# A graph network's first pass over the edges: later scans of a block's sums, and another deal of the last block's columns between TensorE and GpSimd

## The chip, the cores and the metric

The kernel runs on one core of a Trainium2 chip. The metric is the device time of one execution in microseconds (us), as the median of several runs.

## The reference

6250 nodes with 16 features each are joined by 200,000 edges, given as `src` and `dst`, with `dst` in ascending order. Four layers follow each other; after each, the layer's result is added to `x`, and the rows are normalised. Cut to what the kernel's passes over the edges do:

```python
x = _layernorm(x + segment_sum(tanh(x[src] * edge_weight[:, None]), dst))           # layer 0: first pass
x = _layernorm(x + edge_attention(x, edge_attr_16, W_msg, W_attn, src, dst))        # layer 1: another kind of loop
h = segment_max(x[src] * edge_weight1, dst);  x = _layernorm(x + h @ W.T + b)       # layer 2: second pass
h = relu(gin_conv(x, ...));  h = gin_conv(h, ...)                                   # layer 3: third and fourth pass,
x = _layernorm(x + log_softmax(h))                                                  #   each a segment_sum(x[src], dst)
```

## The kernel before

**The layout.** 125 partitions hold 1600 consecutive edges each (`P` = 125, `J` = 1600), so one column of edges is 125 edges, one per partition. A pass (`edge_scan`, called four times, for layers 0, 2, and twice for layer 3) goes through 8 blocks (`NB`) of 200 columns (`JB`). For each block it fills a tile `xb` with the 16 features of every edge's source node, multiplies by weights where the layer has them (`message`; in the first pass with ScalarE's tanh after it), runs 16 scans along the columns, one per feature (`pieces`, L554 and L557), and stores the running sums (`keep_rows`) to DRAM, from where the values at each node's last edge are gathered later (`at_nodes`).

**Two ways to fetch the features.** GpSimd (POOL) fetches a column by an indirect DMA (`gather`, L100), one instruction for each column, all issued at the start of a block (L573 and L574). TensorE (PE) fetches the others by products: `one_hot` (L487; in the first pass its fourth part is made on ScalarE, L491 and L492) turns 12 columns of keys into one-hot matrices, `select` multiplies them for four columns at a time with the table of nodes in three bf16 parts and four groups of columns (48 matmuls, L523), and VectorE (DVE) picks the right entry out of PSUM with a product and a reduction (`kept`, L527, and L532). A batch is 12 columns (`BC`), three `select` calls, 144 matmuls. `select` has three PSUM buffers, `xb` has two.

**Who fetches what.** In blocks 0 to 6, PE fetches the first 120 columns (`NPE`, ten batches) and POOL the last 80. In block 7, the batches are dealt over the block: of every 16 columns (`LW`), PE fetches 12 and POOL 4, over 12 batches in the first pass (`more` = `MORE` = 24 columns on top of 120), over 11 in the second, over 10 in the last two. Columns after the last batch are POOL's. So POOL fetches 56 columns of block 7 in the first pass.

**The order of work.** The order of instructions is written out by hand (`tc.manual_schedule()`). Within the loop over batches, batch c = 0 of a block first issues POOL's gathers into a new `xb` buffer; these wait until the scans of the block two before have read that buffer. The block that was filled before is kept in `waiting`; its `message` stands at c = 2 of the next block (L580), and its 16 scans and its store follow in `todo`, two after each `select` from c = 3 on, so that they end at c = 5 (L602 to L605). Block 7 is scanned in parts, since nothing comes after it: at c = 5 the columns up to there (0 to 64), at the last batch the columns from 64 to that batch's first (176), and the rest after the loop (L586 to L615). `sc`, which the scans write, has one buffer; the next block's scans wait for its store.

**Work beside the first pass.** `prelude` attaches other steps of the program to the `select` calls of the first pass, by number (`at(k, ...)`, three numbers to a batch): keys of the later blocks (`keys_made`), the ends of the nodes' edges (with 51 gathers on POOL at number 50), rows of edges for layer 1 (`edge_rows`, from number 19 on, in steps), 50 scatters on POOL at number 102 (`chunks_put`), the chunk steps at 150 to 168 (`chunks_got` to `chunks_use`), and weights of later layers at 172 to 188.

Of the kernel before, what the change touches and what calls it, by code (L numbers as in the profile page):

```python
# [25 lines left out]
NB = J // JB  # L26
# [6 lines left out]
NPE = 120  # L33
GP = 125
BC = 12
MORE = 24
KEYED = NB * NPE + MORE
LW = 16
SG = 4
GROUPS = ((0, 13), (26, 12), (38, 12), (13, 13))  # L40
GR = len(GROUPS)
# [9 lines left out]
def tile_gnn_resnorm(ctx: ExitStack, tc: tile.TileContext, a: dict, out: bass.AP):  # L51
# [185 lines left out]
    def keys_made(sp, b):  # L237

        w = NPE if b < NB - 1 else NPE + MORE
        df = sp.tile([P, w], F32, name="key_df")  # L240
# [68 lines left out]
    def by_target(t):  # L309
        return t[bass.ds(half, E), :]  # L310
# [184 lines left out]
    def edge_scan(tag, table, parts, F, message, pen, tmp, beside=None, first=None, more=0):  # L495
# [7 lines left out]
        shared = beside is not None  # L503
# [4 lines left out]
        with tc.tile_pool(name=f"es_{tag}", bufs=3) as ep, \  # L508
# [4 lines left out]
            batches = [(b, c) for b in range(NB) for c in range(len(batches_of(b, more)))]  # L513
            lasts = len(batches_of(NB - 1, more)) - 1

            def select(xb, j, oh, k, c):

                all_ps = gp.tile([128, SG // 2, 512], F32, name="all_ps")
                for i in range(SG):
                    for g, (a0, n) in enumerate(GROUPS):  # L520
                        o = all_ps[:, i // 2, (i % 2) * W:(i % 2) * W + n * F]
                        for q in range(3):
                            nc.tensor.matmul(o, oh[:, g, (c + i) * P:(c + i) * P + 128],  # L523
                                             parts[:, q, a0:a0 + n, :].rearrange("p a f -> p (a f)"),
                                             start=(g == 0 and q == 0), stop=(g == GR - 1 and q == 2))
                kept = ep.tile([P, SG, GA, F], F32, name="kept", bufs=1)
                nc.vector.tensor_tensor(  # L527
                    kept.rearrange("p (h i) a f -> p h (i a) f", i=2),
                    all_ps[:P, :, :2 * W].rearrange("p h (i f) -> p h i f", f=F),
                    place1[:, k * BC + c:k * BC + c + SG, :].rearrange("p (h i) a -> p h (i a)", i=2).unsqueeze(3).to_broadcast(  # L530
                        [P, SG // 2, 2 * GA, F]), op=OP.mult)
                nc.vector.tensor_reduce(xb[:, j:j + SG, :], kept.rearrange("p i a f -> p i f a"), AX.X, OP.add)  # L532
# [34 lines left out]
            prev, todo, waiting = None, [], []  # L567
            for k, (b, c) in enumerate(batches):
                if c == 0:
                    xb_all = ep.tile([128, JB, F], F32, name="xb", bufs=2)  # L570
                    xb = xb_all[:P]
                    at = batches_of(b, more)
                    for j in sorted(set(range(JB)) - {j + i for j in at for i in range(BC)}):  # L573
                        gather(xb_all[:GP, j, :], table, src_all[:GP, b * JB + j:b * JB + j + 1])  # L574
                oh = ohs
                if keys:
                    ohs = one_hot(ep, keys.pop(0), shared=shared)
                if k + 2 < len(batches):
                    keys.append(load_keys(ep, k + 2))
                if c == 2 and waiting:  # L580
                    xw, bw = waiting.pop(0)
                    message(xw, bw, 0, JB)
                    sc, last = scans(bw, prev)
                    prev, todo = sc, pieces(xw, bw, sc, last, 0, JB)
                    todo.append(lambda sc=sc, bw=bw: keep_rows(sc, bw, 0, JB))
                if b == NB - 1 and c in (5, lasts):  # L586

                    while todo:
                        todo.pop(0)()
                    if c == 5:  # L590
                        sc, last = scans(b, prev)
                        lo, hi = 0, at[c - 1]
                    else:
                        lo, hi = hi, at[c]
                    message(xb, b, lo, hi)
                    todo = pieces(xb, b, sc, last, lo, hi)
                    todo.append(lambda lo=lo, hi=hi: keep_rows(sc, b, lo, hi))
                for i in range(0, BC, SG):
                    for do in beside.pop((k * BC + i) // SG, ()):
                        do()  # L600
                    select(xb, at[c] + i, oh, k, i)
                    if c > 2:  # L602
                        for do in todo[:6 if b == NB - 1 and c == lasts else 2]:
                            do()
                            todo.remove(do)  # L605
                if k + 1 == len(batches) or batches[k + 1][1] == 0:
                    while todo:
                        todo.pop(0)()
                    waiting.append((xb, b))
# [193 lines left out]
    def chunks_got(tmp, n, got):  # L803

        for i in range(n, min(n + 2, NC)):
            also = tmp.tile([128, Q, 4], F32, name="ck_also" if i else "ck_got", bufs=2 if i else 1)
            nc.sync.dma_start(also, chunk_d[i].rearrange("(p t) c -> p t c", t=Q))
            if i:
                nc.vector.tensor_max(got, got, also)
            else:  # L810
                got = also
        return got

    def chunks_last(tmp, got, cur):

        for f in range(4):
            nc.vector.tensor_tensor_scan(cur[:, :, f], got[:, :, f], got[:, :, f], 0.0, op0=OP.max, op1=OP.max)
        tail = tmp.tile([128, 4], F32, name="ck_tail")
        nc.vector.tensor_copy(tail, cur[:, Q - 1, :])
        nc.vector.tensor_scalar(nost, tail[:, 0:1], 0.0, None, op0=OP.is_equal)  # L820
        return tail

    def chunks_tail(scratch, tail):
        tail_ps = scratch(4, 128)
        nc.tensor.transpose(tail_ps, tail, ident)
        return tail_ps

    def chunks_run(tmp, tail_ps):
        tails = tmp.tile([4, 128], F32, name="ck_tails")
        nc.vector.tensor_copy(tails, tail_ps)  # L830
        run = tmp.tile([4, 129], F32, name="ck_run")
        nc.vector.memset(run[:, 0:1], 0.0)
        nc.vector.tensor_tensor_scan(run[:, 1:], tails, tails, 0.0, op0=OP.max, op1=OP.max)
        return run

    def chunks_before(scratch, run):
        before_ps = scratch(128, 4)
        nc.tensor.transpose(before_ps, run[:, :128], ident[:4, :4])
        return before_ps
# [54 lines left out]
    def attention_weights(tmp):  # L894
        w = tmp.tile([NK, D, 2, D], F32, name="w_am")
        for q in range(3):
            for k, n in enumerate(("attn", "msg")):
                nc.sync.dma_start(w[q * D:(q + 1) * D, :, k, :], a[f"L1_gnn_W_{n}"].rearrange("e (i o) -> e i o", o=D))
        for k, n in enumerate(("attn", "msg")):
            nc.sync.dma_start(w[3 * D:NK, :, k, :], a[f"L1_gnn_b_{n}"].rearrange("(x i o) -> x i o", x=1, o=D))  # L900
        return w

    def attention_parts(tmp, w):
        w_m = tmp.tile([NK, 2 * DD], BF16, name="w_m")
        nc.vector.memset(w_l, 0.0)
        w = w.rearrange("e i k o -> e (i k o)")
        split3(nc.vector.tensor_copy, w_h[:NK, :], w_m, w_l[:NK, :], w, w)
        nc.sync.dma_start(w_h[NK:, :], w_m)
        nc.vector.tensor_copy(identb, ident)
# [36 lines left out]
    def prelude(kp, more):  # L946
# [6 lines left out]
        now = {}  # L953

        def at(k, do):
            jobs.setdefault(k, []).append(do)
# [9 lines left out]
        def open_pool(name):  # L966
            stack.close()
            now["sp"] = stack.enter_context(tc.tile_pool(name=name, bufs=1))

        def put(**what):  # L970
            for k, f in what.items():
                now[k] = f
# [40 lines left out]
        at(100, lambda: put(c=chunks_set(now["sp"], *now["c"])))  # L1013
        at(102, lambda: chunks_put(*now["c"]))
        for i in range(0, NC, 2):
            at(150 + i, lambda i=i: put(got=chunks_got(now["sp"], i, now.get("got"))))
        at(160, lambda: put(c=chunks_last(now["sp"], now["got"], now["raw"])))
        at(163, lambda: put(c=chunks_tail(scratch, now["c"])))
        at(164, lambda: put(c=chunks_run(now["sp"], now["c"])))
        at(167, lambda: put(c=chunks_before(scratch, now["c"])))  # L1020
        at(168, lambda: chunks_use(now["sp"], now["got"], now["raw"], now["c"]))
        at(172, lambda: open_pool("weights"))
        at(172, lambda: put(w=attention_weights(now["sp"])))
        at(176, lambda: attention_parts(now["sp"], now["w"]))
        for i in range(3):
            at(180 + 4 * i, lambda i=i: node_weights(i))
        at(20, lambda: store(nc.sync, ew, by_target(ew_d).rearrange("(p j) o -> p (j o)", j=J)))
        at(14, lambda: put(r=edge_rows_begin(now["rp"])))
        for i in range(J // WE):
# [184 lines left out]
    with tc.tile_pool(name="l1t", bufs=1) as lp, tc.tile_pool(name="l1tp", bufs=1, space=PSUM) as pp:  # L1214
# [12 lines left out]
        for h in range(2):  # L1227
# [16 lines left out]
            now = lp.tile([128, 128], F32, name="now", bufs=2)  # L1244
# [240 lines left out]
```

## Time and profile before

| what | value |
|---|---|
| median of 8 runs | 8196.98 us (8185.38 to 8218.49) |
| the profiled execution's own time | 8247.67 us |
| its span, from first to last instruction | 8245.9 us |
| granted TensorE clock, mean | 0.958 |
| PE busy | 7207.2 us (87%) |
| DVE busy | 6757.2 us (82%) |
| POOL busy | 5803.9 us (70%) |
| ACT busy | 2158.3 us (26%) |
| first pass | 29.9 to 1348.1 us |
| layer 1 | 1348.1 to 4547.1 us |
| second, third and fourth pass | 4547.1 to 5756, to 6981, to 8245.9 us |

All times within the kernel are from one profiled execution, whose own time is 50.7 us above the median of the runs. An engine's busy share over the whole span is an average over stages with different limits, so the first pass has to be read for itself. "Idle before" a group of instructions, or a wait in the list of waits, names what ended the wait; "issue" means that the profile shows nothing that the engine waited for. PE's matmuls are pipelined, so a busy PE is not PE at its peak: the count of matmuls in a stretch tells the pace. Some matmul records can be missing.

### The profile page before, as it was taken

To read this page: it belongs to the slowest core of one execution; us is meant where nothing else is said; L and a number is where in the kernel's file an instruction comes from. 1 tells how busy PE (TensorE), PEld (TensorE's weight loads), DVE (VectorE), ACT (ScalarE), POOL (GpSimd) and SP (SyncE) were. 2 spreads that over 40 slices of the span, in tenths; PEclk is the share of its full clock that TensorE was granted. 3 is DMA by queue.
4 is the path that set the end of the run, shared out by engine and by line. 5 is a ranking of instruction groups with operands and counts; after the bars stand their busy time and mean duration, and the time that the engine had idled before them with its cause. 6 is when DMAs were issued, how large, how long until landed. Compare 5 with 4: busy or idle time off the path is not lost. (4 is left out here: it accounts for less than half of the span.)

```text
span 8245.9 us, 134767 instructions
## 1 busy us (share of the span) xinstructions
PE 7207.2 (87%) x56019; PEld 5194.4 (63%) x56019; DVE 6757.2 (82%) x7894; ACT 2158.3 (26%) x3387; POOL 5803.9 (70%) x4870
## 2 busy tenths in 40 slices
PE   7888895699999999999995899995999996999995
PEld 6786785244444444444442788985888885788884
DVE  8797875699999999999998687876687875677875
ACT  2343331355555555555555000000000000000000
POOL 6888753777777777777773787772787673877673
PEclk9999997899999999999997999997999997999997
DMA  4343432111211222221213122221222221122221
GB/s 132 88 108 91 105 84 72 39 49 49 52 49 49 50 51 50 51 52 49 52 49 124 35 50 41 50 40 31 37 50 41 49 42 35 31 50 40 49 41 29
DMA packets 288780, 461.34 MB, mean 56 GB/s; under 512 B 134741, under 2 KB 187270, under 8 KB 284358
## 3 DMA queue, kind: packets, MB, share of 16 engines
q1 hardware_dynamic: 122818, 332.42, 12.0%
q0 software_dynamic: 164880, 105.68, 11.0%
q10 hardware_dynamic: 448, 14.40, 0.5%
q8 instruction: 445, 7.29, 0.4%
q14 instruction: 189, 1.55, 0.1%
HBM read 257.45 MB, written 206.15 MB: 56 GB/s over the span
## 5 line engine op out<-in xcount | busy, mean ns | idle before, releaser
L523 PE MATMUL all_ps<-parts,oh 125*128 125x208 bf16 (+1 forms) x46512 | 4393.9, 250 | 365.4 <-issue 142.6
L523 PEld LDWEIGHTS <-oh 125*128 125x128 bf16 x46512 | 3945.3, 98 | 813.2 <-issue 724.0
L100 POOL DMA_INDIRECT hg<-table_x,g x1760 | 2024.2, 1150 | 546.2 <-issue 514.5
L100 POOL DMA_INDIRECT xb<-table_x,src x1268 | 1595.4, 1258 | 539.0 <-issue 413.9
L527 DVE TENSOR_TENSOR kept<-all_ps,place 125x832 f32<-125x832 f32 x969 | 986.1, 1018 | 897.1 <-remote 783.9
L1146 PE MATMUL la<-e,ident 128*128 128x512 f32 x3520 | 1576.5, 601 | 4.5 <-DVE e L1133 3.8
L532 DVE TENSOR_REDUCE xb<-kept 125x64 f32<-125x832 f32 x969 | 1521.1, 1570 | 33.3
L1146 PEld LDWEIGHTS la<-e,ident 128*128 128x128 f32 x3520 | 659.5, 193 | 753.2 <-issue 746.2
L1098 DVE TENSOR_TENSOR e<-mm,hg 128x1024 f32<-128x1024 f32 x880 | 1016.3, 1210 | 126.9 <-remote 80.6
L100 POOL DMA_INDIRECT xb<-table_l3b,src x640 | 793.3, 1240 | 301.4 <-issue 216.4
L100 POOL DMA_INDIRECT xb<-in_x,src x616 | 787.1, 1278 | 265.2 <-issue 232.2
L1093 PE MATMUL mm<-w_h,eT 98*128 98x512 bf16 x1760 | 675.3, 384 | 340.5 <-DVE e L1098 155.6
L1110 ACT ACTIVATE e<-e,epen 128x256 f32<-128x256 f32 x1760 | 786.8, 500 | 134.9 <-issue 98.6
L487 DVE TENSOR_SCALAR oh<-keys,mykey 125x1504 bf16<-125x1504 uint16 x1202 | 741.2, 676 | 46.7 <-DMA keys<-key_d 27.6
L1094 PE MATMUL mm<-w_l,eT 98*128 98x512 bf16 x1760 | 677.1, 385 | 1.9 <-issue 1.9
L1126 ACT ACTIVATE e<-e 128x1024 f32<-128x1024 f32 x440 | 464.9, 1057 | 719.4 <-DVE e L1124 553.1
L1094 PEld LDWEIGHTS <-eT 98*128 98x128 bf16 x1760 | 171.0, 97 | 707.0 <-issue 600.3
L1124 DVE TENSOR_TENSOR e<-e,st 128x1024 f32<-128x1024 f32 x440 | 519.5, 1221 | 7.7
L1133 DVE TENSOR_TENSOR e<-e 128x1024 f32<-128x1024 f32 x440 | 516.6, 1214 | 0.0
L100 POOL DMA_INDIRECT g<-edges_d,eidx x220 | 235.6, 1071 | 283.4 <-DVE each L634 140.1
L478 ACT ACTIVATE ln_s<-ln_s,eps_t 125x35 f32<-125x35 f32 (+1 forms) x8 | 2.5, 315 | 1305.1 <-DVE ln_s L477 1242.4
L1086 ACT COPY eT<-tr 98x1024 bf16<-98x1024 bf16 x220 | 222.6, 1012 | 460.1 <-remote 231.0
(371 smaller groups left out, 3673.2 us busy)
## 6 DMA issues: line engine op xcount, KB each, us to landing
keys<-key_d SPq DMA_DIRECT2D x321, 367.2 KB
rows_l<-st SPq DMA_DIRECT2D x220, 384.0 KB
edges_d<-er_t SPq DMA_DIRECT2D x64, 546.9 KB
hg<-table_x,g POOLq DMA_INDIRECT x1760
xb<-table_x,src POOLq DMA_INDIRECT x1268
rows_l<-sc SPq DMA_DIRECT2D x14, 1400.0 KB
ef_d<-in_edge_attr ACTq DMA_DIRECT2D x8, 1562.5 KB
er_ef<-ef_d SPq DMA_DIRECT2D x64, 175.0 KB
```

Of the source, the lines that this page charges most:

```text
L100: nc.gpsimd.indirect_dma_start(out=dst_ap, out_offset=None, in_=table, in_offset=bass.IndirectOffsetOnAxis(ap=idx, axis=0))
L487: nc.vector.tensor_scalar(oh[:, g, :], keys, mykey[:, g:g + 1], None, op0=OP.is_equal)
L523: nc.tensor.matmul(o, oh[:, g, (c + i) * P:(c + i) * P + 128], parts[:, q, a0:a0 + n, :].rearrange("p a f -> p (a f)"), start=(g == 0 and ...
L527: nc.vector.tensor_tensor(kept.rearrange("p (h i) a f -> p h (i a) f", i=2), all_ps[:P, :, :2 * W].rearrange("p h (i f) -> p h i f", f=F), ...
L532: nc.vector.tensor_reduce(xb[:, j:j + SG, :], kept.rearrange("p i a f -> p i f a"), AX.X, OP.add)
L1093: nc.tensor.matmul(ps[:, i, :], eT[:, s + i, :], w_h, start=True, stop=False)
L1094: nc.tensor.matmul(ps[:, i, :], eT[:, s + i, :], w_l, start=False, stop=True)
L1098: nc.vector.tensor_tensor(e[:, s:s + 2, :].rearrange("p s (i x) -> p (s i) x", x=2 * D), ps.rearrange("p s (i x) -> p (s i) x", x=2 * D), ...
L1110: nc.scalar.activation(part(e, 0)[:, k], part(e, 0)[:, k], AF.Identity, bias=epen[:, t, k:k + 1])
L1124: nc.vector.tensor_tensor(sc, sc, top.rearrange("p (i o) -> p i o", o=D).unsqueeze(1).to_broadcast([128, 4, D, D]), op=OP.subtract)
L1133: nc.vector.tensor_tensor(part(e, 1)[:, s:s + 4], part(e, 1)[:, s:s + 4], part(e, 0)[:, s:s + 4], op=OP.mult)
L1146: nc.tensor.matmul(ps, ident, e[:, s, :], start=(s == 0), stop=False)
```

## The change

First, the deal of block 7: `MORE` grows from 24 to 48 and `LW` shrinks from 16 to 14. In the first pass block 7 has 14 batches, and PE fetches 168 of its columns, 12 of every 14; POOL fetches 32. `LW` holds for all passes: in the others PE fetches as many columns as before, but they lie closer together, so that the first column of the last batch is 140 for 160 in the second pass and 126 for 144 in the last two.

Second, the first pass alone (`shared`): from block 3 on, the waiting block's `message` and scans stand at c = 8 of the next block, where they stood at c = 2, and three pieces follow each `select` for two. Block 7 is scanned from its start only at its last batch, in one piece of 182 columns, and then the rest.

Third, the steps of `prelude` from number 150 on move to numbers 25 higher.

```diff
-MORE = 24
+MORE = 48
 KEYED = NB * NPE + MORE
-LW = 16
+LW = 14
...
+            late, parted = (8, (lasts,)) if shared else (2, (5, lasts))
...
-                if c == 2 and waiting:
+                if c == (late if b > 2 else 2) and waiting:
                     xw, bw = waiting.pop(0)
                     message(xw, bw, 0, JB)
...
-                if b == NB - 1 and c in (5, lasts):
+                if b == NB - 1 and c in parted:
                     while todo:
                         todo.pop(0)()
-                    if c == 5:
+                    if c == parted[0]:
                         sc, last = scans(b, prev)
-                        lo, hi = 0, at[c - 1]
+                        lo, hi = 0, at[c - 1] if c < lasts else at[c]
                     else:
                         lo, hi = hi, at[c]
...
                     if c > 2:
-                        for do in todo[:6 if b == NB - 1 and c == lasts else 2]:
+                        for do in todo[:6 if b == NB - 1 and c == lasts else 3 if shared else 2]:
...
         for i in range(0, NC, 2):
-            at(150 + i, lambda i=i: put(got=chunks_got(now["sp"], i, now.get("got"))))
+            at(175 + i, lambda i=i: put(got=chunks_got(now["sp"], i, now.get("got"))))
...
-        at(168, lambda: chunks_use(now["sp"], now["got"], now["raw"], now["c"]))
-        at(172, lambda: open_pool("weights"))
+        at(193, lambda: chunks_use(now["sp"], now["got"], now["raw"], now["c"]))
+        at(197, lambda: open_pool("weights"))
...
-            at(180 + 4 * i, lambda i=i: node_weights(i))
+            at(205 + 4 * i, lambda i=i: node_weights(i))
```

More of the change, by code (lines that the diff above doesn't have):

```diff
@@ L1015, in prelude @@
         for i in range(0, NC, 2):
-            at(150 + i, lambda i=i: put(got=chunks_got(now["sp"], i, now.get("got"))))
[L1017 to L1020, printed above, removed]
-        at(168, lambda: chunks_use(now["sp"], now["got"], now["raw"], now["c"]))
-        at(172, lambda: open_pool("weights"))
-        at(172, lambda: put(w=attention_weights(now["sp"])))
-        at(176, lambda: attention_parts(now["sp"], now["w"]))
+            at(175 + i, lambda i=i: put(got=chunks_got(now["sp"], i, now.get("got"))))
+        at(185, lambda: put(c=chunks_last(now["sp"], now["got"], now["raw"])))
+        at(188, lambda: put(c=chunks_tail(scratch, now["c"])))
+        at(189, lambda: put(c=chunks_run(now["sp"], now["c"])))
+        at(192, lambda: put(c=chunks_before(scratch, now["c"])))
+        at(193, lambda: chunks_use(now["sp"], now["got"], now["raw"], now["c"]))
+        at(197, lambda: open_pool("weights"))
+        at(197, lambda: put(w=attention_weights(now["sp"])))
+        at(201, lambda: attention_parts(now["sp"], now["w"]))
         for i in range(3):
-            at(180 + 4 * i, lambda i=i: node_weights(i))
+            at(205 + 4 * i, lambda i=i: node_weights(i))
         at(20, lambda: store(nc.sync, ew, by_target(ew_d).rearrange("(p j) o -> p (j o)", j=J)))
```

## The prediction

> **What bounds the kernel now.** Blocks are numbered b = 0 to 7 and batches c = 0 upwards, as in the code; a batch is three `select` calls, 144 matmuls. I read the page first, then the sums by stage, because the change is almost wholly in the first pass (29.9 to 1348.1 us). The columns are: stretch, its length, busy time (count) of PE, PEld, DVE, ACT, POOL, then granted clock, DMA share and GB/s.
>
> ```profile
> 29.90:1348.10 1318.20, 1158.42 (x11927) 1021.31 (x11927) 1086.69 (x1527) 446.17 (x441) 905.70 (x713) 0.98 0.40 97
> ...
> 652.40:736.50 84.10, 66.68 (x566) 46.88 (x566) 42.66 (x49) 22.78 (x24) 67.32 (x56) 0.98 0.30 62
> 424.00:474.90 50.90, 47.26 (x524) 44.23 (x524) 50.48 (x67) 25.23 (x25) 41.07 (x33) 1.00 0.48 119
> ...
> 1232.10:1331.00 98.90, 98.76 (x1152) 98.61 (x1150) 87.60 (x105) 21.08 (x14) 0.00 (x0) 1.00 0.13 46
> 1153.40:1208.20 54.80, 47.12 (x445) 36.26 (x443) 30.97 (x34) 17.68 (x17) 43.95 (x36) 1.00 0.32 66
> ```
>
> No engine is full over the pass. The four short stretches are whole batches, and give the paces that carry the forecast. With no gather on POOL, eight batches take 98.9 us: 12.4 each. With gathers and no scans on DVE, three take 54.8: 18.3 each (21.0 where scatters and edge rows run as well, 652 to 736). With gathers and a block's scans, four take 50.9: 12.7 each, DVE then being full (50.5). The clock is 0.98 to 1.00 in all, so it isn't the clock. The waits of the first pass say who loses the time:
>
> ```profile
> PEld L523 <- issue: 260.6, 654, 11.3
> POOL xb L100 <- issue: 232.2, 607, 28.4
> DVE kept L527 <- remote: 168.5, 59, 5.6
> ...
> DVE sc L557 <- DMA rows_l<-sc: 3.5, 1, 3.5
> ```
>
> PE loses 260 us in small gaps that no semaphore explains, and DVE waits for PE. The DVE timeline of one such batch (block 3, c = 8) shows it:
>
> ```profile
> 675.04 1.02 DVE L527 TENSOR_TENSOR kept<-all_ps,place 125x832 f32<-125x832 f32 x1 [1.65 <-remote]
> ...
> 683.35 1.02 DVE L527 TENSOR_TENSOR kept<-all_ps,place 125x832 f32<-125x832 f32 x1 [5.60 <-remote]
> ...
> 690.85 1.02 DVE L527 TENSOR_TENSOR kept<-all_ps,place 125x832 f32<-125x832 f32 x1 [4.40 <-remote]
> ...
> 698.37 1.02 DVE L527 TENSOR_TENSOR kept<-all_ps,place 125x832 f32<-125x832 f32 x1 [2.40 <-remote]
> ```
>
> That is 23.3 us for a batch for which DVE needs some 11. Prices come from the view of tile xb, and POOL's idle times from its timeline:
>
> ```profile
> L532 DVE TENSOR_REDUCE xb<-kept x969: 1545/1570/1605, 40.3 to 8137.9; 125x64 f32<-125x832 f32 x194
> L100 POOL DMA_INDIRECT xb<-in_x,src x616: 1205/1209/3555, 23.0 to 1210.0; - x154
> L557 DVE TENSOR_TENSOR_SCAN sc<-keep,last,xb x336: 321/614/671, 437.5 to 8115.2; 125x200 f32<-125x200 f32 x144, 125x64 f32<-125x64 f32 x24
> ...
> L942 DVE TENSOR_TENSOR xb<-xb,ew x10: 537/3478/3554, 236.1 to 1344.1; 125x3200 f32<-125x3200 f32 x7, 125x1024 f32<-125x1024 f32 x1, 125x1792 f32<-125x1792 f32 x1, 125x384 f32<-125x384 f32 x1
> ```
>
> ```profile
> 968.01 1.21 POOL L100 DMA_INDIRECT xb<-in_x,src  x1 [19.32 <-issue]
> ...
> 1125.17 1.21 POOL L100 DMA_INDIRECT xb<-in_x,src  x1 [28.40 <-issue]
> ...
> 1210.03 1.21 POOL L100 DMA_INDIRECT xb<-in_x,src  x1 [0.30 <-issue]
> 1351.30 0.97 POOL L100 DMA_INDIRECT g<-edges_d,eidx  x1 [140.06 <-DVE each L634]
> ```
>
> A gather costs POOL 1.21 + 0.30 = 1.51 us, a block of 80 so 121 us. POOL waits twice (19 and 28 us), for the `xb` buffer that the scans of the block two before have to release, and is done 140 us before the pass ends. POOL does not bound; its gathers matter by what PE loses while they run.
>
> **The change, part by part.**
>
> *Two more batches.* 24 columns are 2 batches; they stand at the end, where no gather runs: 2 x 12.4 = +24.8 us on PE. DVE needs 2 x (3 x (1.02 + 1.57) + 3 x 0.68) = 19.6, ACT and the keys' load less; all lie beside PE. `keys_made` works on 168 columns for 144: L258 grows by 24/120 of 1.78 = 0.4, its fifteen small steps by 0.04 each: +1 on DVE, in batch 41.
>
> *24 gathers less.* 36.2 us of POOL. On the path they are worth between nothing (POOL ends early anyhow) and 36.2 x (1 - 12.4/18.3) = 11.7, the pace that PE gets back. I take 10, since the gathers of block 7 run beside plain batches (1153 to 1208). So the dealing alone costs +16.
>
> At this point the Trainium skill (SBUF — State Buffer, § Who interferes with whom) says the opposite of the rows: a DMA never contends with a compute engine. By it a batch would take 12.4 with gathers or without, their removal would be worth 0, and the dealing +26. The rows (18.3 against 12.4) differ, and the measurement decides.
>
> *Later scans.* From block 3 on, message (3.48) and 16 scans (16 x 0.61) leave c = 2 to 5 for c = 8 and 9, nine pieces per batch. The DVE work is the same, 13.3 us per block. What moves is the release of `xb`: gathers of block b + 1 may start only at the end of block b, and not after c = 5. They then run beside plain batches (18.3), and the scans run with no gather, so the cheap pairing (12.7) is lost. Block by block, a batch's time being taken from one batch's first L527 to the next:
>
> Blocks 1 and 2: three pieces per select, same DVE work: 0.
>
> Block 3: before, 174.2 us. c = 1 to 5 (18.7, 10.8, 20.2, 20.6, 12.7) are DVE-bound and lose 13.3 of DVE work; PE's pace with gathers lets at best that through. c = 7 to 9 (22.6, 23.3, 19.8) have 33.7 us of idle DVE and take the work for nothing. I take -8 (bounds -33, if these also fell to 15, and 0).
>
> Block 4: before, 163.2. Its gathers wait for the end of block 3 instead of starting at 695; 121 us at 18.3 is 6.6 batches; the other 3.4 include the scans, 14.3 of DVE work each: 169, or 165 if PE starts fresh. +4.
>
> Blocks 5 and 6: before, 155.3 and 153.3. After a pause of POOL the trace shows about two batches at full pace (13.1 and 10.6 after 1125, then 18.3): 24.8 us; 96 us at 18.3 are 5.3 batches; 2.7 remain. The chunk steps, moved by 25 places, put c = 8 and 9 of block 5 at 18.3 and 16.2 us of DVE, and batch 64 (`chunks_use`) at 21.2; the batches that they leave (16.3, 14.0, 23.6) fall to the plain pace. 121 + 44 = 165 and 121 + 40 + 3 = 164: +10 and +11. The queued `chunks_got` loads and weight DMAs go to SP behind the keys' loads, and the first reader is far on: 0.
>
> Block 7: before, 151. 32 gathers hold 48 us (3.3 batches), 10.7 more at 12.4 are 133; scans at c = 7 to 9 exceed 12.4 by 2; the last batch has message and scans of 182 columns for 112: +4. The 3.5 us wait of L557 for the store of block 6 goes, since its store is then long done. 187, so +36, the two batches and the 24 gathers included.
>
> Sum by blocks: -8 + 4 + 10 + 11 + 36 = +53.
>
> *The same by the whole pass.* Before, (616 + 51 + 50) gathers and scatters x 1.51 = 1083 us of 1311 with POOL on; the 228 off hold 18.4 batches, so 63.6 on: 17.0 each. After, 693 x 1.51 = 1046 hold 61.5; 22.5 remain, at 12.4 = 279: 1325, +14. This grants that the lost pairing costs nothing. I take the middle, +36 (34, and the lost pairing is what the rows show).
>
> *The other passes.* `LW` also deals their last block 12 of 14, so more columns wait for the tail: 60 for 40 in the second, 74 for 56 in the last two. Scans of 80 and 56 columns differ by 0.065 us, so 16 scans grow by 0.8, less 0.4 from the shorter piece before, and the last store grows by a third of 2.5 us: +1 each, +3.
>
> In all +39: on the profiled execution 8247.67 (span 8245.9 and 1.8 around it) gives 8287; that execution lies 50.7 above the median of the runs, 8196.98, which gives 8236.
>
> **The rivals.** *A: only totals count* (same, 0.14). PE's pace follows the number of gathers, wherever the scans lie: +14 + 3 and down to 0 if the DVE-bound batches of block 3 gain more: 8197 to 8214. For it: 17.0 is steady over the pass. Against: 12.7 beside 18.3.
>
> *B: idle DVE is filled* (faster, 0.13). DVE-heavy batches bound the pass: 31, 33, 34, 41, 53 and 55 (123.8 us) fall to their new DVE work, 88.4: -35; 58, 59 and 64 give back 15; 37 to 39 go from 65.7 to 43 as scans do with gathers: -23; the dealing +16, the tails +3: -24, 8173. It decides if batches stripped of scans keep 12.7 with gathers on. Against: plain batches with gathers took 18.3 to 23.3.
>
> *C: the bursts are all slow* (within the forecast's side). If the bursts of blocks 4 to 6 run at 21.0, 5.8 batches in 121 us and 4.2 at 14 make 180 each: +85, 8282.
>
> *D: it does not do what it says.* The buffer release could be later still only if block 7's gathers passed c = 13; they end near c = 3. I give it nothing.
>
> **How the numbers follow.** 0.2% is 16.4 us, about what a measurement of this kernel can tell from no change. Slower (above 8213): forecast and C, 0.73; same: A, 0.14; faster: B, 0.13. The range leaves B out below and C's end above: 8188 to 8282. The forecast's own range is 8214 to 8270.
>
> **What would show it.** Right: POOL idle for 20 to 45 us before the gathers of blocks 5, 6 and 7, each starting at a block's end; batches of c = 1 to 7 in blocks 5 and 6 mostly at 15 to 18; c = 8 and 9 near their DVE work; a pass that ends 25 to 55 later. Wrong: plain batches with gathers at 13 or less (B), or a pass end unmoved but for some 15 us (A).

## The result and the profile after

The change made the kernel slower: 8253.06 us (median of 11 runs, 8218.56 to 8264.46) against 8195.77 for the kernel before beside it (32 runs), a ratio of 1.0062 [1.0047, 1.0077]. The profiled execution took 8319.1 us (span 8317.0); it lies 66 us above its median, as the one of before lay 51 above its own. The spans differ by 71.1 us:

| stretch | before | after | difference |
|---|---|---|---|
| first pass, to its last block's end | 1348.1 | 1399.2 | +51.1 |
| nodes of layer 0, layer 1's loop, to the last `la` product | 3101.2 | 3103.5 | +2.3 |
| layer 1's finish, to the second pass's first `kept` | 105.7 | 115.4 | +9.7 |
| second to fourth pass | 3690.9 | 3698.9 | +8.0 |

The sums by stage of the kernel after follow; the columns are as before. The first row is the first pass, the second block 6, the third and fourth are plain batches with gathers, the fifth two batches of scans with hardly a gather, the last three batches with none.

```profile
core 0: us, PE busy (x) PEld busy (x) DVE busy (x) ACT busy (x) POOL busy (x), PEclk, DMA share, GB/s
29.90:1399.20 1369.30, 1187.17 (x12215) 1055.17 (x12215) 1099.36 (x1526) 452.33 (x444) 864.55 (x689) 0.97 0.38 93
...
1038.20:1211.10 172.90, 143.00 (x1445) 123.83 (x1443) 133.66 (x193) 60.04 (x61) 100.33 (x81) 0.96 0.37 85
...
750.50:805.30 54.80, 45.80 (x411) 33.22 (x410) 32.70 (x38) 18.86 (x21) 43.76 (x36) 1.00 0.37 77
916.50:955.10 38.60, 32.53 (x292) 23.25 (x292) 21.59 (x25) 10.62 (x12) 30.83 (x26) 1.00 0.34 70
837.20:866.20 29.00, 28.94 (x338) 28.79 (x337) 28.80 (x41) 13.77 (x13) 1.05 (x1) 1.00 0.28 81
...
1267.10:1304.10 37.00, 37.00 (x434) 37.00 (x432) 27.76 (x28) 9.29 (x6) 0.00 (x0) 1.00 0.09 32
```

The paces came as forecast: 18.3 and 19.3 us a batch with gathers and no scans (12 and 13 gathers each), 14.5 with scans and no gathers, DVE being full (28.80 of 29.00), and 12.3 with neither. POOL's timeline shows the new order: the first gathers of blocks 5, 6 and 7 each start at a block's end after 40 to 51 us of idle time (20 to 45 were forecast).

```profile
865.15 1.22 POOL L100 DMA_INDIRECT xb<-in_x,src  x1 [39.99 <-ACT oh L492]
...
1037.12 1.23 POOL L100 DMA_INDIRECT xb<-in_x,src  x1 [50.93 <-ACT oh L492]
...
1210.04 1.22 POOL L100 DMA_INDIRECT xb<-in_x,src  x1 [48.49 <-ACT oh L492]
```

So far this is nearly the forecast; only the batches c = 1 to 7 of blocks 5 and 6, put mostly at 15 to 18 us, lie wider apart, from 12.5 to 22.7. But DVE is busy 12.7 us more (1099.36 for 1086.69) and idle 38.4 us more, and the list of its waits says for whom. First before, from 471 us to the pass's end, then after, over the same stretch (times in all, count, longest; lines under 1 us are left out, and "remote" means that the profile names no engine):

```profile
DVE kept L527 <- remote: 123.9, 41, 5.6
DVE kept L527 <- PE all_ps L523: 10.1, 10, 1.5
DVE er_ef L720 <- issue: 5.6, 2, 2.8
DVE er_ef L720 <- ACT er_t L717: 3.7, 1, 3.7
DVE sc L557 <- DMA rows_l<-sc: 3.5, 1, 3.5
DVE er_ef L720 <- DMA er_ef<-ef_d: 2.3, 1, 2.3
```

```profile
DVE kept L530 <- remote: 123.3, 42, 5.6
DVE kept L530 <- PE all_ps L526: 17.2, 14, 1.5
DVE er_ef L723 <- issue: 10.8, 2, 6.0
DVE ck_got L812 <- DMA ck_also<-chunk_d: 10.0, 1, 10.0
DVE oh L487 <- issue: 8.5, 1, 8.5
DVE er_ef L723 <- ACT er_t L720: 6.5, 1, 6.5
DVE er_ef L723 <- DMA er_ef<-ef_d: 6.0, 1, 6.0
DVE oh L487 <- DMA keys<-key_d: 1.1, 1, 1.1
```

Waiting for PE (the `kept` lines: `kept` reads what PE wrote) grew by 6.5 us only, from 134.0 to 140.5. The other lines, but for the 3.5 us for the store, are waits of instructions that read what SP, the engine that issues loads and stores, has loaded (rows of edges, by way of ACT or not, chunk rows, keys); for some the profile names no releaser and puts "issue". They grew from 11.6 to 42.9, by 31.3. These sums hide that the blocks go different ways. Taken from one block's first `kept` to the next one's (block 7 to the pass's end), before and after, in us:

| blocks | length | DVE busy | DVE waits for PE | DVE waits for loads |
|---|---|---|---|---|
| 3 and 4 | 337.4, 321.3 | 261.9, 259.7 | 64.8, 46.1 | 6.5, 11.3 |
| 5 and 6 | 308.6, 344.9 | 257.5, 256.3 | 43.8, 69.2 | 2.3, 16.0 |
| 7 | 158.1, 188.1 | 135.5, 153.3 | 18.6, 21.5 | 0, 9.6 |

In blocks 5 and 6 both kinds of wait grew, that for PE by 25.4 and that for loads by 13.7; in blocks 3 and 4 DVE waited 18.7 less for PE. Of the 42.9 us, 31.0 lie in the first batches of blocks 4, 5, 6 and 7 (6.5, 6.0, 10.0 and 8.5), right behind a block's store in SP's queue. In the same four batches before, DVE waited for PE instead, 28.7 us, and so the batches themselves are hardly longer: 17.2, 16.6, 21.7 and 18.7 us for 18.3, 17.9, 16.7 and 18.2, 3.1 in all. Around block 6's start, SP's issues and DVE's instructions read so:

```profile
1036.27 0.32 SPq L96 DMA_DIRECT2D rows_l<-sc  x1
1036.63 0.40 SPq L97 DMA_DIRECT2D rows_l<-sc  x1
1037.08 1.06 SPq L282 DMA_DIRECT2D keys<-key_d  x1
1038.34 1.60 SPq L96 DMA_DIRECT2D er_ef<-ef_d  x1
1040.14 2.84 SPq L97 DMA_DIRECT2D er_ef<-ef_d  x1
1043.09 0.45 SPq L810 DMA_DIRECT2D ck_also<-chunk_d  x1
```

```profile
1039.24 1.58 DVE L535 TENSOR_REDUCE xb<-kept 125x64 f32<-125x832 f32 x1
1050.83 1.16 DVE L812 TENSOR_TENSOR ck_got<-ck_got,ck_also 128x956 f32<-128x956 f32 x1 [10.01 <-DMA ck_also<-chunk_d]
```

The store waits for the last scan; the keys, edge rows and chunk rows stand behind it and are issued in one go after it; DVE then stands still for 10 us. With early scans the same store stood in the middle of the block, with loads behind it as well, and the waits in the batch that followed (c = 6) were 0 to 3.7 us in blocks 3 to 6.

### The profile page after: what moved, and what is told of

It reads as the page before. It is cut to its first block, busy times and chain, and to the rows that moved or that the text cites. A ratio compares the mean times of both kernels' runs of the same rounds, so it can differ in the third digit from the quotient of the medians.

```text
span 8317.0 us, 135329 instructions
## 1 busy us (share of the span) xinstructions
PE 7242.3 (87%) x56307; PEld 5231.3 (63%) x56307; DVE 6771.7 (81%) x7895; ACT 2164.2 (26%) x3390; POOL 5754.3 (69%) x4846
## 5 line engine op out<-in xcount | busy, mean ns | idle before, releaser
L526 PE MATMUL all_ps<-parts,oh 125*128 125x208 bf16 x46800 | 4427.4, 250 | 384.5 <-issue 133.9
L100 POOL DMA_INDIRECT xb<-in_x,src x592 | 742.3, 1254 | 353.9 <-issue 177.1
L1096 PE MATMUL mm<-w_h,eT 98*128 98x512 bf16 x1760 | 674.3, 383 | 337.4 <-DVE e L1101 163.6
L1097 PEld LDWEIGHTS <-eT 98*128 98x128 bf16 x1760 | 170.7, 97 | 703.4 <-issue 595.6
L1096 PEld LDWEIGHTS <-eT 98*128 98x128 bf16 x1760 | 171.8, 98 | 272.3 <-issue 93.0
```

The source lines that it names most:

```text
L100: nc.gpsimd.indirect_dma_start(out=dst_ap, out_offset=None, in_=table, in_offset=bass.IndirectOffsetOnAxis(ap=idx, axis=0))
L1096: nc.tensor.matmul(ps[:, i, :], eT[:, s + i, :], w_h, start=True, stop=False)
L1097: nc.tensor.matmul(ps[:, i, :], eT[:, s + i, :], w_l, start=False, stop=True)
```

## The experiments

They ran in four groups, each on a chip of its own beside the kernel before. That kernel took 7560.1, 7561.4 and 7561.7 us in the first three groups and 7682.9 in the fourth, where it had taken 8196 in the comparison above. So something is quicker in the groups, and times are compared within a group alone.

### The deal alone

```diff
-MORE = 24
+MORE = 48
...
-LW = 16
+LW = 14
```

> The new deal alone (MORE = 48, LW = 14); scans, pieces per select and chunk steps stay as in the kernel before. Theory P (the prediction's: what a gather costs TensorE depends on what VectorE does beside it, so the later scans cost by the lost pairing): +16 us against before (10 to 26), all of it in block 7 and after batch 70 of the first pass. Rival A (only the totals of batches and gathers count): the whole of the change's +51, since the totals are the same as in the changed kernel.

7597.97 us, +37.9, ratio 1.0055 [1.0041, 1.0069]. It lies between the two theories. Set beside the profile of the kernel with held gathers below, whose time equals before's, the difference of 37 is: first pass +23.1 (1244.6 for 1221.5), layer 1's finish +10.5, the later passes +3.5. So the two batches cost about what was said (23.1 for 24.8), the 24 gathers fewer were worth next to nothing, the tails cost the +3 of the prediction, and 10 us in layer 1 were in nobody's sum.

### Later scans and moved steps alone

The other parts of the change, with `MORE` = 24 and `LW` = 16.

> The later scans and the moved chunk steps alone (MORE = 24, LW = 16 as before; block 7 in one piece up to its last batch). Theory P: +20 to +45 us: block 3 of the first pass shorter by some 15, block 4 the same, blocks 5 and 6 longer by some 15 to 20 each. Rival A: 0, within 10, since not one gather or batch is added.

7562.8 us, ratio 1.0004 [0.9995, 1.0013]: rival A's number, though not by its reason, as the waits below show.

### Early scans, late gathers

```diff
+                    if shared and b > 3:
+                        nc.vector.memset(xb_all[:GP, 12 if b == NB - 1 else NPE, :], 0.0)
```

> The kernel before, with the gathers of blocks 4 to 7 of the first pass held back until their own block begins (a VectorE memset of one column of the new xb buffer, 16 elements, which the first gather must wait for); the scans stay at c = 2 to 5, so they run beside the gathers. GpSimd starts as late as in the changed kernel. Theory P (the pairing counts, not the start): within -20 and +10 us of before. Rival R (the later start of the gathers is itself what costs): +20 to +45, as with the later scans.

7561.43 us, ratio 1.0001 [0.9992, 1.0010]: within theory P's range and outside the rival's. It says little, because on this chip the lost pairing has no price to begin with. Three plain batches with gathers (in the run of the deal alone) take 10.6 us each, DVE being full, where the first comparison's took 18.3:

```profile
316.70:348.50 31.80, 31.80 (x374) 31.80 (x372) 31.43 (x37) 17.10 (x18) 25.40 (x22) 1.00 0.52 129
```

Here the waits of DVE from 480 to 1220 us are worth reading. First this kernel, then the one with later scans:

```profile
DVE xb L944 <- DMA xb<-in_x,src: 26.3, 1, 26.3
DVE kept L527 <- PE all_ps L523: 12.9, 12, 1.5
DVE ck_got L811 <- DMA ck_also<-chunk_d: 9.4, 3, 5.1
DVE er_ef L722 <- ACT er_t L719: 7.9, 3, 2.8
DVE sc L557 <- DMA rows_l<-sc: 4.4, 1, 4.4
```

```profile
DVE kept L530 <- PE all_ps L526: 24.0, 24, 1.5
DVE er_ef L723 <- ACT er_t L720: 16.1, 3, 6.1
DVE ck_got L812 <- DMA ck_also<-chunk_d: 10.3, 3, 9.7
DVE oh L487 <- DMA keys<-key_d: 5.6, 1, 5.6
```

With early scans, the `message` at c = 2 of block 5 waits 26.3 us for block 4's last gather: POOL, which also did 51 gathers and 50 scatters for other work, is the late one. It isn't late because its gathers were held: in the run of the deal alone, which holds none, the same wait is 24.8. Later scans remove that wait and the 4.4 for the store. They give back 11 in waits for PE and 14 in waits for SP's loads. In the first comparison the 26.3 us did not exist (the list of before above has no such line), so there, by this reading, only the giving back was left; the later scans alone were not run under its conditions.

### One-hots spread over the batch

The kernel before, with the last two of a batch's one-hot instructions on DVE moved behind the first and second `select`.

> The kernel before, with the four one-hot instructions of the next batch dealt over the batch (two at its start, one after each of the first two selects; in the first pass one and one and one) instead of all at its start. No work is added. In the trace TensorE keeps 17 or 18 matmuls per gather for some 6 us after these instructions, and 11 or 12 from then on until they come again; the gather beside them takes 1.45 us for 1.21. Theory L (an instruction of VectorE that holds up a gather sets TensorE free for some 6 us, scans do the same, and that is the pairing): plain batches with gathers fall from 15.4 us to 12.5 to 13.5 in the last three passes and from 18.3 to some 15 in the first, the whole by 150 to 350 us. Rival I (it is idle VectorE as such, or the keys' transfer that follows): no change within 30 us, or slower by as much as TensorE can run ahead less.

7609.59 us, ratio 1.0064 [1.0050, 1.0078]: theory L's gain did not come, and the kernel is 49.5 us slower. But the loss that it was to cure is hardly there in this group (10.6 us for a plain batch with gathers, not 18.3), so the theory isn't tested for the conditions of the first comparison. Why the kernel is slower shows in PE's waits for the one-hots; in the kernel with held gathers the same line has 0.2 us:

```profile
PE all_ps L528 <- DVE oh L488: 139.6, 69, 11.7
```

### The changed kernel again, and with room in memory

```diff
-        zero = cp.tile([128, RW], F32, name="zero")
+        zero = tail
```

> The changed kernel itself, beside the others of this group. If the kernel before takes some 7560 us here, as in the first group (deal alone +38 us by the medians, later scans alone +3), theory P (the two parts add up) expects +36 to +44, ratio 1.005 to 1.006. Where the kernel before takes some 8200 us, it expects what the first comparison gave, +51 to +57 in the first pass and layer 1's finish. Rival: the parts interact, because the deal's two batches stand where later scans would have left room; then it is under +30 or over +55 where the kernel before takes 7560.

> The changed kernel, with the tile zero of layer 1 (3072 bytes a partition) put into tail, which is free until layer 1's end: no computation changes. Theory M (memory): MORE = 48 makes place1 312 bytes a partition larger (24 columns of 13), the tiles of the second pass's first one-hot no longer fit beside layer 1's, and so these four instructions and the keys' load move from the start of layer 1 into its finish, where DVE's and ACT's order changes and 10 us are lost. With 3072 bytes given back, the four instructions run at layer 1's start again and the stretch from the last la product to the first kept of the second pass is 10 us shorter than in the changed kernel (105 against 115): the time is 8 to 12 us under f1_after. Rival S: the 10 us come from the deal of the columns itself or from run to run differences; then the time is within 4 us of f1_after, or the stretch is unchanged.

The changed kernel took 7595.23 us, +33.8, ratio 1.0044 [1.0030, 1.0058], a little under the sum of its parts (37.9 and 2.8): below theory P's +36 to +44 and not as low as the rival's +30, so neither is borne out. With room it took 7583.11, ratio 1.0029 [1.0018, 1.0039]. Theory M holds: 12.1 us less by the medians, and the stretch in layer 1's finish went from 115.6 to 105.3. (The two profiled spans differ by 4.0 only, since the first pass of the second was 3.9 longer.) In the changed kernel, the one-hots of the second pass's first batch run in that stretch, at 4230.80, and ACT then waits for other things, in another order:

```profile
4230.80 2.42 DVE L487 TENSOR_SCALAR oh<-keys,mykey 125x1504 bf16<-125x1504 uint16 x4 [1.58 <-DMA keys<-key_d]
```

```profile
ACT L1306 <- DMA r<-rows_l,idx_row: 18.6, 4, 12.7
ACT now L1249 <- DVE now L1248: 13.1, 1, 13.1
```

With room they run at layer 1's start, from 1333.0 on, and ACT's waits in the finish are these:

```profile
ACT L1306 <- DMA r<-rows_l,idx_row: 10.0, 4, 6.0
ACT now L1249 <- DMA fx<-rows_l,fix_row: 9.2, 1, 9.2
...
ACT now L1249 <- DVE now L1248: 4.7, 1, 4.7
```

`place1` grows with `MORE` by 24 columns of 13 bytes. That was enough to push a tile that another layer prefetches into a later free place.

### Fewer columns for TensorE

```diff
-    rows, carry = edge_scan("l0", ..., prelude(kp, MORE), more=MORE)
+    rows, carry = edge_scan("l0", ..., prelude(kp, BC), more=BC)     # 0, 0 in the first of the two
```

> The kernel before, with 24 columns of the first pass's block 7 taken from TensorE and given to GpSimd (the opposite of the change's deal): ten batches and 80 gathers in block 7. The deal +24 cost +23 in the first pass of the first group, two batches at 12.4 less 0 for the gathers. Theory P where the kernel before takes some 8200 us: -25 for the batches, +0 to +12 for the gathers, so -25 to -13. Where it takes 7560: GpSimd ended its 56 gathers there some 45 us before the pass did, and 24 more take 36, while the pass would be 25 shorter; GpSimd then ends about 15 us after the last batch began to be the end, and the last scans of 56 columns follow: -5 to +10. Rival: the gathers are never late, -23 on either.

> The kernel before, with 12 columns of the first pass's block 7 taken from TensorE and given to GpSimd: eleven batches and 68 gathers in block 7. Theory P: one batch less, -12.4, and 12 gathers more worth 0 to +6, GpSimd not being late in either place (it ends 18 us later, having had 45 or more): -6 to -13, a version that beats both kernels by 0.1%. Rival: what f3_none shows is a late GpSimd already here, 0 to +5.

With ten batches: 7562.39 us, ratio 1.0002 [0.9993, 1.0011], as theory P had it for this chip. The last `kept` came at 1187.7, but POOL's last gather at 1209.5, and the pass ended at 1218.2. With eleven: 7551.76, ratio 0.9987 [0.9978, 0.9996]; the last gather at 1189.7 was in time, and the pass ended at 1210.2. So of the deals tried here (ten, eleven, twelve and fourteen batches) eleven is the best in these groups: a batch costs some 12, a gather next to nothing until POOL is last.

> Twelve columns less for TensorE in the first pass's block 7 (as in the run with eleven batches) and twelve less in the second pass's (ten batches, as in the third and fourth). Theory P: a second batch of 12.4 goes, and 12 gathers more in the second pass are worth 0 to +6, since the third and fourth pass run with the same 80 gathers a block: -19 to -25 against the kernel before, 0.997, and the second pass (first kept to the tails' copy) takes 998 for 1010. Rival: the second pass's message stands ahead of its last scans and GpSimd is late there: -5 to -12 as with the first pass alone.

7551.02 us, ratio 0.9986 [0.9977, 0.9995]: no better than eleven batches in the first pass alone. The rival is right. The second pass took 1011.6 for 1009.7 in the run with eleven batches, because its `message` had to wait for the gathers:

```profile
DVE xb L1363 <- DMA xb<-table_x,src: 13.7, 1, 13.7
```

### No gathers

> The kernel before, in which blocks 2 to 6 of the first pass get no gathers: one memset of the 80 columns stands for each block's, so those columns' features are left out, and nothing else. By the prices of the prediction (plain batches 18.3 with gathers, 12.4 without), 400 gathers of 1.51 are 604 us, and their removal is worth 604 x (1 - 12.4 / 18.3) = 195 us at most, and some 100 with the batches that DVE bounds taken out. Theory P' (where the kernel before takes 7560, PE keeps its pace beside gathers, and the deal's two batches therefore cost +23 and its gathers nothing): the first pass is within 15 us of the kernel before's, 1205 to 1235 against 1220. Rival: the gathers cost there too, and later scans came out even for another reason: 30 to 100 us less.

7516.09 us in one run; the first pass ended at 1178.2, 43 us earlier than the 1221.5 of the kernel with held gathers (in another group), so theory P' missed its bound and the rival's range holds. But 26.6 of the 43 are one batch, the one with the 26.3 us wait for the last gather (43.6 and then 17.0); the other 16.7 are spread thin, most of it as some 0.3 us a batch over blocks 2 to 6. So on these chips gathers take next to nothing from PE; what they cost is being late.

### The store out of the loads' way

The later scans and moved steps alone, and:

```diff
+                if c == 1 and held:
+                    held.pop(0)()
...
-                    todo.append(lambda sc=sc, bw=bw: keep_rows(sc, bw, 0, JB))
+                    (held if shared and 2 < b < NB - 1 else todo).append(lambda sc=sc, bw=bw: keep_rows(sc, bw, 0, JB))
```

> The later scans and moved steps alone, as in the run of them that came out even (7562.8), with one thing more: the store of a block's sums, which stands behind the last scans at the block's end, is issued at c = 1 of the next block, behind that batch's load of keys. In the run before, SP waited 102.8 us in seven stores for DVE's scans, and the loads of keys, of edge rows and of chunk rows stood behind it in its queue; DVE then lost 31 us in waits for those loads (ck_got 10.3, er_ef 16.1 by way of ACT, oh 5.6), against 18 with early scans, and the late scans' gain, 26.3 us of waiting for gathers at c = 2 of block 5, was eaten. Theory Q (the queue behind the store eats it): DVE loses 10 to 20 us less, and the kernel takes 7542 to 7553 where the kernel before takes 7561. Rival W (the loads are late by the store's own 1.6 MB on the DMA engines, or PE's pace, not the wait, bounds these batches): within 5 us of 7562.

> The same with eleven batches in block 7 of the first pass for twelve (12 columns from TensorE to GpSimd). The fewer columns alone gave -10 and GpSimd ended its gathers 30 us before the pass; Theory Q and the deal add up: 7530 to 7544, the best of all. Rival: with the scans of block 6 and block 7 at the end, the last gathers come late or the last scans are the bound: no better than j1_store.

7665.58 us where the kernel before took 7682.85: ratio 0.9976 [0.9966, 0.9987], 17 us less, as theory Q had it (8 to 19 less), against 1.0004 without the edit. The intervals lie apart, but the two ratios are of two chips, and on this one the later scans were not run without the edit, so how much of the 17 the store is worth isn't shown. The waits bear theory Q out: DVE's waits for loads in the same stretch were 32 us and are now 9:

```profile
DVE kept L530 <- remote: 33.0, 22, 2.9
DVE kept L530 <- PE all_ps L526: 15.0, 15, 1.9
DVE er_ef L725 <- ACT er_t L722: 5.7, 1, 5.7
...
DVE ck_got L814 <- issue: 2.5, 1, 2.5
DVE ck_got L814 <- DMA ck_also<-chunk_d: 1.0, 1, 1.0
```

The first batches of blocks 4 to 7, in the run of the later scans and in this one, went from 16.7, 16.9, 21.5 and 15.8 us to 10.8, 10.6, 11.7 and 10.2. The run doesn't part the late issue of the loads from the store's own bytes: the loads now go ahead of both. With eleven batches as well it is 7662.23, 0.9973 [0.9961, 0.9985]; the 3.4 us between the two are within their intervals and less than the 10 expected, so the rival (no better with eleven batches than with twelve) isn't excluded.

## Why the prediction was right, and where its steps were not

**The direction and the time.** Slower was forecast, with 8236 in a range of 8188 to 8282, which is +39; 8253 was measured, +57. In the profiles, the first pass took 15 more than the +36 put down for it, and layer 1's finish 9.7 more than the nothing put down for it. The rows of the forecast appeared: gathers in bursts from a block's end, 18.3 us a batch beside them, scans alone at DVE's pace.

**The choice of the middle.** The sum by blocks said +53 for the first pass; +51.1 was measured. The term that was mis-sized is the halfway point of +36 between that sum and the whole-pass sum of +14.

**The blocks.** Block 3 was put at -8 and gave -15.8, block 4 at +4 and gave -0.3, blocks 5 and 6 at +10 and +11 and gave +16.7 and +19.6, block 7 at +36 and gave +30. Blocks 5 and 6 came out 15 above their terms, the other three 18 below: that the sum came so near is luck.

**The loads in blocks 5 and 6.** This is the step that failed, although the number stood. The prediction wrote that the loads on SP's queue stand behind others and "the first reader is far on: 0". The readers stood in the very next batch, where DVE waited 6.0 us in block 5 and 10.0 in block 6. The first two batches of each block, put at 24.8 us together, took 29.1 and 35.1. These 14.6 us are about the 15 by which the two blocks missed. The forecast moved a block's scans to its end and did not ask what else that moves: the store behind the last scan went along, and with it every load queued after.

**PE beside the gathers.** The loss that was forecast was there in these blocks: DVE's waits for PE grew by 25.4 us. Over blocks 3 to 7 they grew by 9.6 only, since blocks 3 and 4 got 18.7 back where scans ran in batches that had waited for PE. In that sum rival A was nearer than the prediction; for where the time goes, it was not.

**What the late loads cost.** In the first comparison this isn't shown. Against the kernel before, the four batches in which they fall took 3.1 us more. Against the 10.2 to 11.7 us that such batches take with the store moved, in the fourth group, it would be 31, an estimate across two chips. The moved store was not tried under the conditions of the first comparison, where PE's slower pace could take a part of the gain back.

The Trainium skill (Perfetto Trace Analysis, § Optimization Strategy) says to take the gaps on the engine at issue, within one stretch, and to find what each gap waits for. Over the whole pass the two lists of DVE's waits account for 34.3 of the 38.4 us of new idle time (31.3 + 6.5, less 3.5 for the store), and seem to say that only the loads matter. Taken by stretch, as in the table by blocks, they show the loss beside the gathers as well.

**The dealing.** Two batches at 12.4 were right (12.4 and 12.2 in the trace of after). The 24 gathers were put at -10; in the first group they were worth next to nothing, and the dealing cost +23 in the first pass. The rule of the Trainium skill (SBUF — State Buffer, § Who interferes with whom) that a DMA never contends with a compute engine, which would have made it +26, came closer there. In the first comparison the row with gathers (18.3) speaks against it, and no run there did the dealing alone.

**The 10 us in layer 1's finish.** Missed. The prediction costed `MORE` by instructions and never by bytes.

**The later passes.** +3 was forecast; +3.5 was measured with the deal alone, in the first group. The +8.0 of the first comparison is larger, but it is made of +16 in the third pass and -10 in the fourth, which have the same code and the same deal, so it is mostly scatter between two executions.

**Rival B.** In the first comparison its condition failed (18.3 us a batch beside gathers). In the first group it held (10.6), and the later scans still came out even: they removed a wait for a late gather, 26.3 us, which rival B did not name, and gave most of it back. With the store out of the way, in the fourth group, the later scans and moved steps do make the kernel faster than before.

**Left open.** The moved steps were not run without the later scans, so their own share isn't known. The granted clock in the first pass was 0.97 for 0.98 before; its share isn't told apart. Why PE keeps its pace beside gathers in one group and not in the first comparison isn't known either.

## What to carry to other kernels

When a step is moved, list what is issued behind it on every queue, and ask of the instruction at its end (here a store that waits) what stands behind that: here SP issued in order, and one late store made the loads of the next block late. Where a constant makes a table longer, ask which tile no longer fits beside it, since a prefetch that loses its place moves into another stage's critical chain. And read the waits of the engine that does the moved work by releaser and block by block, before and after: a sum that comes out right may be made of terms that are wrong both ways, and a sum of waits over a pass can hide blocks that go opposite ways.

## What the runs showed of the hardware

The kernel before took 8196 us in the first comparison, 7560 to 7562 on three chips and 7683 on another, at a like mean granted clock (0.958 in its profile, 0.961 in that of the kernel with held gathers, whose time equals its own in the first group). In the passes' matmuls, PE's weight loads sat idle for 724.0 us with nothing in the profile to wait for in the first of these profiles, and for 130.3 in the second:

```profile
PEld L523 <- issue: 724.0, 2182, 13.2
```

```profile
PEld L523 <- issue: 130.3, 51, 29.5
```

In the first these are 2182 gaps for 51. A price such as "18.3 us a batch beside gathers" held for that execution's conditions and not for the kernel.
